# Eighty presorted chunks in place of sixty-three in a graph-convolution kernel on one core

## The chip, the core and the metric

The kernel runs on one core of one Trainium2 chip. The number that counts is the device time of one execution in microseconds (us). Three runs of the kernel before took 5122.73, 5125.78 and 5127.1 us; the median is 5125.78 us. One more execution, of 5141.47 us, was recorded by the hardware profiler; every row of a profile below is of that one.

A core has five engines, each with its own queue of instructions that it works off in order: TensorE (PE, matmuls; PEld is its loading of weights), VectorE (DVE), ScalarE (ACT), GpSimd (POOL) and SyncE (SP, which here issues DMAs only). They wait for each other through semaphores.

## The reference

412,500 edges, sorted by destination `dst`, carry 20 features and a weight; 12,500 nodes carry 128 features. Cut to what matters:

```python
h    = relu(layernorm(x)) @ W_in2f
Wij  = (ssp(f_ij @ W_f1 + b_f1) @ W_f2 + b_f2) * rcut_ij[:, None]
x_ij = h[dst] * Wij                        # the message of an edge
agg  = segment_sum(x_ij, src, 12500)       # messages added up by source node
out  = x + ssp(agg @ W_o1 + b_o1) @ W_o2 + b_o2
```

`ssp` is softplus minus log 2. The edges come in the order of `dst`, so that `h[dst]` is nearly local; `src` is random, so that adding up by `src` is the hard part. The nodes lie in 98 blocks of 128 (`NBLK`).

## The kernel before

**Chunks and steps.** The edges are cut into 806 chunks of 512 (`NCH`), and a chunk into four tiles of 128 edges (`QT`). A Python function `step(k)` writes the instructions of one step of the pipeline; what it writes is the order on every engine (the schedule is manual). The order inside a step is the string `"TMHPRXEBCKSAVUZWJL"`, a letter for each part: M is the product of value and picked node (line 1069, one DVE instruction for each chunk, the best clock of the steps), H the scaling of the picked rows on ACT (1056), P picks `h[dst]` with four matmuls (1040), R ranks the edges of a chunk (949, 921 on PE, 929 on DVE), X is one piece of the presort, C and S are the compares and the matmuls of the collection (1171, 1193), A and V make the value (1007, 1019), Z the hidden layer (878, or 874 for a sorted chunk), L its logarithm on ACT (884, 491, 492). Parts run ahead of their chunk: P of step k belongs to chunk k+2, Z to chunk k+4 at most, the loads of rows to chunk k+6 (`LW`).

**A chunk that is not sorted.** Its messages are scattered to a table in DRAM, so that the messages of one source block lie together: POOL issues four indirect DMAs for each chunk (1085), 128 rows of 129 floats each. The place of a row comes from the rank of its edge in its block, for which DVE marks the blocks (900), PE counts them (949, 921) and DVE takes the maximum (929). The first scatter of a chunk waits for a signal of PE in a later step (`PACED`).

**Segments and tiles.** The chunks form seven segments (`SEGS`; chunks 0 to 351, 352 to 527, 528 to 647, 648 to 703, 704 to 759, 760 to 791, 792 to 805). Each has a table with `T` tiles of 128 rows for each of the 98 blocks, and one more for the blocks whose own chunks lie in it. `T` is worked out from the mean number of messages of the chunks that are not sorted, with a margin of four standard deviations, and rounded up. When a segment is complete, its table is collected: SP loads a unit of up to six tiles (1151), DVE compares the stored place of each row with 0 to 127 (1171), and PE adds each tile into its block with one matmul (1193; it stands twice in a trace, since a 32-bit matmul is recorded as two). Segment 0 is collected from step 363 on. A small planner spreads all this work evenly over the steps that are left (`rate`, `jobs`): before, 9.12 tiles for each step in steps 371 to 658, 9.4 in 659 to 770, 10.9 in 771 to 804, and the rest behind the last chunk.

**A sorted chunk.** Some chunks (`SORT`, 63 of them: 57, 61, 65, ... 341, every fourth chunk, with a gap of eight after six or seven of them) are sorted by source block beforehand. The generator `sorting()` does it, piece by piece, four steps for each chunk, from step `PRE` = 18 on: PE ranks the 512 edges and permutes features, places and windows with matmuls against one-hot matrices (1372 to 1403), DVE makes these matrices (1396, 1399), ACT copies the result (1406), SP stores it (`s_rows` in 1407, `s_cols` in 1355, the latter one step later, when the next chunk's sort has begun). When the chunk's turn comes, SP loads the three pieces back (859, 860, 863), the features enter through three 16-bit matmuls (874), and the messages, which already lie in the order of blocks, go to `s_msgs` with one plain DMA of SP (1078). No rank, no marks, no scatters.

**Gathers.** Per block, one indirect DMA of POOL (1138) fetches the rows of that block from all sorted chunks: 128 places, each a run of `GR` = 6 consecutive messages. A chunk has one place by right (63), and where it has more than six edges of the block it takes further places (`EX` = 44 are kept for that). The indices of these runs are made by `indices()` after the last sort (44 DVE instructions in 1468, three in a step). A gather adds six tiles to the work of its block; the 98 gathers are dealt to the segments by their share of tiles (`extras`), and a gather is issued at the earliest four steps after the last sorted chunk and twelve steps before its compare (`EARLY`).

**What sets the order around the change.** The list `SORT` decides which chunks skip the scatter path; through `kept` in `Segment` it sets `T`, and through `T` the planner's `rate` and `jobs`. `PRE` says when the presort begins.

## Time and profile before

| | us |
|---|---|
| three runs | 5122.73, 5125.78 (median), 5127.1 |
| the profiled execution | 5141.47 |
| its span, first to last instruction | 5139.7 |
| PE busy | 3898.2 |
| DVE busy | 3190.8 |
| POOL busy | 3022.7 |
| ACT busy | 2716.1 |
| granted TensorE clock, mean | 0.868 of full speed |

The page gives busy times over the whole span. The span has stages with different work, so the stretches of time are what has to be read: there is one product (line 1069) for each chunk, and the number of these in a window divides its length into steps. The page's part on the chain that ended last is empty for this execution; what bounds a stretch has to be read from windows and waits. In a row of groups stand line, engine, operation, output and inputs, shapes and count; then busy time and the mean of one; then the idle time in front of it and what ended it.

### The profile page before, as it was taken

What the parts mean: (1) busy time and instruction counts of PE and PEld (TensorE: products, weight loads), DVE (VectorE), ACT (ScalarE), POOL (GpSimd) and SP (SyncE); (2) the same over time, 40 slices, a digit from 0 to 9 for tenths busy, and PEclk for the clock granted to TensorE, in tenths of its full rate; (3) what the DMA queues carried; (4) which work ended last, traced back from release to release, by engine and by line L of the source; (5) the groups of instructions that cost most, each with busy time, mean ns of one, the idle gap of its engine ahead of it and who ended that gap; (6) DMA issues with size and microseconds to landing.
All of it is one profiled execution on the core that took longest, in us unless ns stands there. A gap on an engine that the chain in (4) does not pass through costs nothing.

```text
span 5139.7 us, 78367 instructions
## 1 busy us (share of the span) xinstructions
PE 3898.2 (76%) x24234; PEld 2985.5 (58%) x24234; DVE 3190.8 (62%) x7496; ACT 2716.1 (53%) x6890; POOL 3022.7 (59%) x3168
## 2 busy tenths in 40 slices
PE   5677777777676566878888887888888778787879
PEld 3444544454444344666666666666666666666667
DVE  5666666666566444555655655665666666666757
ACT  6556666666666555445445444444444444444423
POOL 5665555555555556666666566666666665666643
PEclk8788888888887778988889898988999999999989
DMA  4556666666554454555565555566555655565647
GB/s 148 157 168 194 184 200 185 179 185 166 142 139 132 136 159 150 180 186 181 183 212 187 174 175 178 172 214 198 175 180 185 214 188 167 180 206 160 198 135 222
DMA packets 570652, 909.02 MB, mean 177 GB/s; under 512 B 160072, under 2 KB 349526, under 8 KB 570224
## 3 DMA queue, kind: packets, MB, share of 16 engines
q1 hardware_dynamic: 466050, 668.14, 43.8%
q0 software_dynamic: 102912, 235.26, 13.9%
q8 instruction: 193, 3.16, 0.3%
q14 instruction: 235, 1.93, 0.1%
q10 hardware_dynamic: 1262, 0.52, 0.0%
HBM read 499.23 MB, written 404.34 MB: 176 GB/s over the span
## 4 chain that ended last, share of the span: by engine, by line


## 5 line engine op out<-in xcount | busy, mean ns | idle before, releaser
L1085 POOL DMA_INDIRECT slots<-o,slot x2971 | 2871.8, 967 | 1885.6 <-issue 1345.1
L884 ACT ACTIVATE a<-z,bf 128x512 f32<-128x512 f32 x806 | 555.9, 690 | 1897.6 <-remote 738.3
L1069 DVE TENSOR_TENSOR o<-v,hg 128x512 f32<-128x512 f32 x806 | 555.2, 689 | 1189.0 <-issue 589.7
L1193 PE MATMUL sums<-to,m 128*128 128x128 f32 x8700 | 1222.8, 299 | 81.0 <-issue 73.2
L1193 PEld LDWEIGHTS sums<-to,m 128*128 128x128 f32 x8700 | 1191.3, 214 | 153.1 <-issue 122.0
L1019 PEld LDWEIGHTS v<-wf,r 128*128 128x128 f32 x6448 | 989.3, 219 | 495.7 <-issue 444.0
L1019 PE MATMUL v<-wf,r 128*128 128x128 f32 x6448 | 995.3, 303 | 36.8 <-issue 31.9
L1056 ACT ACTIVATE hg<-v,rcut 128x128 f32<-128x128 f32 x2972 | 837.6, 365 | 187.7 <-remote 94.2
L878 PE MATMUL z<-f,wf1z 128*128 128x512 f32 x1486 | 844.5, 649 | 61.1 <-issue 42.7
L1171 DVE TENSOR_TENSOR to<-counts,m 128x640 f32<-128x640 bf16 (+4 forms) x812 | 607.2, 782 | 358.8 <-remote 172.6
L1040 PEld LDWEIGHTS <-at 126*128 126x128 bf16 x2964 | 228.8, 104 | 808.2 <-issue 464.7
L1007 PE MATMUL v<-hb 128*128 128x512 bf16 x784 | 336.2, 429 | 352.2 <-DVE o L1069 274.9
L891 DVE SCALAR_TENSOR_TENSOR r<-z,nbf,a 128x512 f32<-128x512 f32 x806 | 598.1, 742 | 2.6 <-ACT a L492 2.1
L492 ACT ACTIVATE a<-a,half 128x512 f32<-128x512 f32 x806 | 581.9, 722 | 26.2
L929 DVE TENSOR_REDUCE top<-counts 128x4 f32<-128x392 f32 x743 | 414.4, 558 | 262.3 <-remote 197.3
L1040 PE MATMUL v<-near,at 126*128 126x128 bf16 x2964 | 321.9, 233 | 321.5 <-DVE at L999 149.5
L491 ACT ACTIVATE a<-a 128x512 f32<-128x512 f32 x806 | 508.0, 630 | 25.5
L949 PE MATMUL counts<-inb,rest_of 128*128 128x392 f16 x736 | 265.8, 361 | 317.5 <-issue 156.5
L878 PEld LDWEIGHTS z<-f,wf1z 128*128 128x128 f32 x1486 | 253.9, 211 | 68.5 <-issue 50.6
L921 PE MATMUL counts<-inb,after 128*128 128x392 f16 x743 | 271.9, 366 | 17.4 <-issue 16.5
L921 PEld LDWEIGHTS <-after 128*128 128x128 f16 x743 | 75.7, 102 | 358.5 <-issue 357.0
L999 DVE TENSOR_SCALAR at<-rel,prow 126x512 bf16<-126x512 bf16 x741 | 268.6, 362 | 0.0
(240 smaller groups left out, 2622.3 us busy)
## 6 DMA issues: line engine op xcount, KB each, us to landing
m<-slots SPq DMA_DIRECT2D x374, 322.5 KB
rel<-rel_d SPq DMA_DIRECT2D x201, 504.0 KB
m<-slots SPq DMA_DIRECT2D x238, 258.0 KB
m<-slots SPq DMA_DIRECT2D x147, 387.0 KB
f<-in_f_t SPq DMA_DIRECT2D x100, 512.0 KB
slots<-o,slot POOLq DMA_INDIRECT x2971
slots<-zero SPq DMA_DIRECT2D x100, 387.0 KB
slots<-zero SPq DMA_DIRECT2D x58, 516.0 KB
```

The lines of the kernel that those rows point to most:

```text
L491: nc.scalar.activation(a, a, AF.Exp, scale=-1.0)
L492: nc.scalar.activation(a, a, AF.Ln, bias=half, scale=0.5)
L878: kept["mm"] = nc.tensor.matmul(z_ps[k % 2], wf1z[:, k, :], self.f, start=True, stop=True)
L884: nc.scalar.activation(self.a[k], z_ps[k % 2], AF.Abs, bias=bf1)
L891: nc.vector.scalar_tensor_tensor(self.r[k], z_ps[k % 2], nbf1, self.a.pop(k), op0=ALU.max, op1=ALU.add)
L1019: mm = nc.tensor.matmul(v[:, i, :], r[:, i * P:(i + 1) * P], wf2, start=False, stop=True, skip_group_check=True)
L1040: mm = nc.tensor.matmul(ps[:, i, :], at[:, i * P:(i + 1) * P], near, start=i == 0, stop=i == QT - 1, skip_group_check=True)
L1056: act = nc.scalar.activation(hg[:, i, :], ps[:, i, :], AF.Copy, scale=cut[:, i:i + 1])
L1069: nc.vector.tensor_mul(self.o[c][:, :, :P], v, hg)
L1085: put = nc.gpsimd.indirect_dma_start(out=views[j % VIEWS], out_offset=bass.IndirectOffsetOnAxis(ap=self.slot[:, j:j + 1], axis=0), in_=o[: ...
L1171: nc.vector.tensor_tensor(to[:, :n, :], count_ps[:, None, :].to_broadcast([P, n, P]), m[:, :n, P:].to_broadcast([P, n, P]), op=ALU.is_equal)
L1193: kept["mm"] = nc.tensor.matmul(self.acc[b // QT][:, i, :], m[:, j, :P], to[:, j, :], start=t == 0, stop=t == self.tiles(b) - 1)
```

## The change

The list of sorted chunks becomes 33, 37, 41, ... 357 (72 chunks, with the same spacing as before) and 365, 373, ... 421 (eight more, every eighth chunk): 80 in all. With them 48 second runs fill the 128 places of a gather exactly. `PRE` goes from 18 to 14. In segment 0, 282 chunks are not sorted where 289 were, in segment 1, 166 where 176 were, and `T` comes out as 13 where it was 14, and as 8 where it was 9; the other segments keep theirs. `GJ`, the number of runs one chunk may have in a block, goes from 6 to 5. `both`, an intermediate, is held in 16 bits, and two small buffers move to another tile, since 80 chunks need more room. The new rule on `extras` gives segment 0 gathers only in even blocks from 62 on, 18 in place of 37; the segments behind it take the others.

```diff
-SORT = tuple(57 + i * 23 // 20 * 4 for i in range(63))
+SORT = tuple(33 + i * 23 // 20 * 4 for i in range(72)) + tuple(365 + 8 * i for i in range(8))
 NS = len(SORT)
 GR = 6
-GJ = 6
-EX = 44
+GJ = 5
+EX = 48
...
+LATE = 62
...
-PRE = 18
+PRE = 14
...
-            first_i = ra[:, 2 * cols:2 * cols + NS].bitcast(I32)
-            first_f = ra[:, 2 * cols + NS:2 * cols + 2 * NS]
...
-            both = rb[:, cols:3 * cols].rearrange("p (c k) -> p c k", k=2)
+            both = rb[:, cols:2 * cols].bitcast(BF16).rearrange("p (c k) -> p c k", k=2)
...
+            first_i = w3[:, 2 * RW:2 * RW + NS].bitcast(I32)
+            first_f = w3[:, 2 * RW + NS:2 * RW + 2 * NS]
...
-            total, start = bank[:nb, 200:201], bank[:nb, 256:256 + NS]
+            total, start = bank[:nb, 220:221], bank[:nb, 256:256 + NS]
...
-            i = max(range(len(share)),
+            i = max((i for i in range(len(share)) if i or b >= LATE and b % 2 == 0),
                     key=lambda i: share[i] * (b + 1) / sum(share) - len(extras[i]))
```

The lines of the changed kernel are one higher than those before, from the constants on.

What the table does to the order is seen in three places. The first is PE in step 31, which picks the rows of chunk 33. Before, behind the last of the four picks (`at` is the window of a chunk that is not sorted) come the two matmuls of the rank, then a piece of the presort (`nall`, `tri`), then bias, value and hidden layer of the next chunks:

```order
L1040 LDWEIGHTS at
L1040 MATMUL v_159<-near,at 128x128
L949 LDWEIGHTS rest_of
L949 MATMUL counts<-inb,rest_of 128x392
L921 LDWEIGHTS after
L921 MATMUL counts<-inb,after 128x392
L1388 LDWEIGHTS nall
L1388 MATMUL sums_158<-tri,nall 128x392
L1007 LDWEIGHTS hb_76
L1007 MATMUL v_160<-hb_76 128x512
L1019 MATMUL v_160<-wf_63,r 128x128 x4
```

In the changed kernel the same place reads (`sorted` is the tile with the presorted data):

```order
L1041 LDWEIGHTS sorted
L1041 MATMUL v_159<-near,sorted 128x128
L1389 LDWEIGHTS nall
L1389 MATMUL sums_158<-tri,nall 128x392
L1008 LDWEIGHTS hb_76
L1008 MATMUL v_160<-hb_76 128x512
L1020 MATMUL v_160<-wf_63,r 128x128 x4
```

The two matmuls of the rank are gone from this step; nothing else moved.

The second place is SP at the first load of sorted data. Before, chunk 57 is loaded (859, 860, 863) behind the store of the sixth sort's columns, so that its own five stores lie far back:

```order
L852 DMA near<-h_2_100 126x128
L1355 DMA s_cols<-pre_1313 128x8
L1921 DMA slots_129<-zero 96x1032
L859 DMA sorted<-s_rows 63x512
L860 DMA sorted<-s_rows 126x1x512
L863 DMA sorted<-s_cols 128x8
L241 DMA xb<-in_x 128x4x128
```

In the changed kernel chunk 33 is loaded directly behind the store of its own columns, the first that there is:

```order
L853 DMA near<-h_1_99 126x128
L1356 DMA s_cols<-pre_1136 128x8
L1922 DMA slots_129<-zero 96x1032
L860 DMA sorted<-s_rows 63x512
L861 DMA sorted<-s_rows 126x1x512
L864 DMA sorted<-s_cols 128x8
L1922 DMA slots_129<-zero 96x1032
L796 DMA f<-in_f_t 128x2x512
```

The load has moved from five sorts behind its own sort to right behind it, with the load of features (`f`) next in the queue.

The third place is PE in step 448, in the stretch in which segment 0 is collected. Before:

```order
L921 LDWEIGHTS after
L921 MATMUL counts<-inb,after 128x392
L1193 MATMUL sums_158<-to,m 128x128 x9
L1007 LDWEIGHTS hb_76
L1007 MATMUL v_160<-hb_76 128x512
L1019 MATMUL v_160<-wf_63,r 128x128 x4
L878 MATMUL z_155<-f,wf1z 128x512
```

And in the changed kernel:

```order
L922 LDWEIGHTS after
L922 MATMUL counts<-inb,after 128x392
L1194 MATMUL sums_157<-to,m 128x128 x8
L1008 LDWEIGHTS hb_76
L1008 MATMUL v_160<-hb_76 128x512
L1020 MATMUL v_160<-wf_63,r 128x128 x4
L879 MATMUL z_155<-f,wf1z 128x512
```

Eight tiles are added in this step in place of nine. Counted over the whole program, 4,468 tiles become 4,272: 297 fewer in steps 363 to 658, 53 more in 659 to 770, 24 more in 771 to 804 and 24 more behind the last chunk. Scatters go from 2,971 to 2,903, the stores and loads of sorted data from 63 to 80 sets.

## The prediction

> **What bounds the kernel now.** I read the page first: no engine is busy for more than 76% of the span, and the chain of waits is empty, so the bound has to be found stretch by stretch.
>
> ```profile
> PE 3898.2 (76%) x24234; PEld 2985.5 (58%) x24234; DVE 3190.8 (62%) x7496; ACT 2716.1 (53%) x6890; POOL 3022.7 (59%) x3168
> PEclk8788888888887778988889898988999999999989
> ```
>
> PE's granted clock steps up in the middle of the span, where segment 0 begins to be collected. So I cut the time at the steps where the work changes: chunks 33 to 56 (sorting has begun, no sorted chunk yet), 57 to 277 (sorted chunks and sorting), 278 to 340 (sorted chunks, no more sorting), 341 to 362 (neither), 371 to 658, 659 to 770 and 771 to 804 (collection at three rates). The windows view of line 1069, one instruction for each chunk, gives the length of a step in each:
>
> ```profile
> 222.30:370.80 148.50, 16.50 (x24) 0.78 0.56 162
> 370.80:1557.10 1186.30, 152.89 (x222) 0.82 0.62 175
> 1557.10:1895.90 338.80, 42.81 (x62) 0.78 0.48 140
> 1895.90:2028.00 132.10, 15.21 (x22) 0.77 0.41 128
> 2077.80:3989.30 1911.50, 198.48 (x288) 0.90 0.58 186
> 3989.30:4742.30 753.00, 77.09 (x112) 0.92 0.60 188
> 4742.30:4981.80 239.50, 23.39 (x34) 0.91 0.52 159
> ```
>
> Columns: window, its length, busy DVE with the count, granted PE clock, DMA share, GB/s. Dividing: 6.19, 5.34, 5.46, 6.00, 6.64, 6.72 and 7.04 us for a step. Two things stand in these rows. Without collection a step costs 6.0 to 6.2 us when no chunk is sorted, and 5.3 to 5.5 when 22% are; whether the presort itself runs (the second row) or not (the third) makes no difference. And with collection a step grows with its tiles, which the same view of line 1193 counts (two records a tile):
>
> ```profile
> 2077.80:3989.30 1911.50, 752.62 (x5272) 734.41 (x5272) 0.90 0.58 186
> 3989.30:4742.30 753.00, 287.64 (x2097) 283.60 (x2096) 0.92 0.60 188
> 4742.30:4981.80 239.50, 104.83 (x746) 101.06 (x747) 0.91 0.52 159
> ```
>
> That is 9.15, 9.36 and 10.97 tiles a step. The windows of all engines and the waits say who sets the pace there:
>
> ```profile
> 1895.90:2028.00 132.10, 81.01 (x373) 53.47 (x373) 58.93 (x138) 70.04 (x176) 83.43 (x86) 0.77 0.41 128
> 2077.80:3989.30 1911.50, 1549.75 (x10182) 1260.66 (x10181) 1153.66 (x2391) 928.53 (x2332) 1170.85 (x1215) 0.90 0.58 186
> ACT a L884 <- remote: 262.4, 61, 7.7
> ACT a L884 <- PE counts L921: 206.5, 68, 6.7
> ACT a L884 <- PE z L878: 202.0, 58, 8.2
> ```
>
> The first two rows give PE, PEld, DVE, ACT and POOL; the other three are waits in the window 2077.8 to 3989.3. In the collection PE is busy 81% (1549.75 of 1911.5), POOL and DVE 61 and 60%; ACT stands for results of PE, and PE is last. Before the collection (first row) nobody is above 63%; a step is a round of waits between PE, DVE, ACT and POOL there.
>
> **The change part by part.** The sum is made against the profiled execution (span 5139.7, whole 5141.5 us); the median of the runs is 0.997 of it, which changes a sum of some 80 us by 0.3, so I subtract from the median directly.
>
> *Sorted chunks before the collection.* Chunks 33 to 56 get six and chunks 341 to 362 four; between 57 and 340 there are 62 where there were 63. I take the step of the mixed stretch, (1186.3 + 338.8) / 284 = 5.37 us: 24 x (6.19 - 5.37) = 19.7, 22 x (6.00 - 5.37) = 13.9, together 33.6. The one chunk lost costs a sorted chunk's worth: 0.63 to 0.82 us a step at 22% sorted is 2.8 to 3.7 us a chunk, say 3.3. Term: **-30 us**. Bounds: 9 chunks net x 2.8 = -25, x 3.7 = -33. The mechanism is not PE's work alone: what a sorted chunk drops is four scatters, the rank and two DVE instructions, against a hidden layer of three 16-bit matmuls:
>
> ```profile
> L1085 POOL DMA_INDIRECT slots<-o,slot x2971 | 2871.8, 967 | 1885.6 <-issue 1345.1 <-PE v L1019 126.1 <-ACT a L884 83.4
> L878 PE MATMUL z<-f,wf1z 128*128 128x512 f32 x1486 | 844.5, 649 | 61.1 <-issue 42.7 <-DVE r L891 14.5 <-DVE inb L900 1.6
> L929 DVE TENSOR_REDUCE top<-counts 128x4 f32<-128x392 f32 x743 | 414.4, 558 | 262.3 <-remote 197.3 <-PE v L1040 18.0 <-issue 17.7
> L921 PE MATMUL counts<-inb,after 128*128 128x392 f16 x743 | 271.9, 366 | 17.4 <-issue 16.5 <-DVE top L929 0.5 <-DVE used L955 0.4
> L949 PE MATMUL counts<-inb,rest_of 128*128 128x392 f16 x736 | 265.8, 361 | 317.5 <-issue 156.5 <-DVE top L929 145.3 <-remote 2.1
> L874 PE MATMUL z<-sorted,wst 63*128 63x512 bf16 x189 | 75.1, 522 | 0.0
> ```
>
> On PE that is 0.37 + 0.36 (rank) and 844.5 / 743 = 1.14 against 75.1 / 63 = 1.19 us: 0.68 us less. The rest of the 3.3 us is the round through DVE (929, for which the next 949 waits 145.3 us in all) and POOL's 3.9 us of scatters.
>
> *Seventeen more sorts.* I cost them at nothing. They fall into steps 278 to 342, and there PE has over a third of its time free (211.27 of 338.8 us busy, first row below); the second and third rows of the first windows show that such free time takes a sort (5.34 with, 5.46 without). If that cover were gone, PE's larger part of a sort,
>
> ```profile
> 1557.10:1895.90 338.80, 211.27 (x1061) 139.32 (x1060) 180.06 (x488) 196.35 (x500) 191.90 (x196) 0.78 0.48 140
> L1403 PE MATMUL sums<-pre,pre_d 128*107 128x512 bf16 x252 | 83.8, 465 | 0.0
> L1377 PE MATMUL sums<-pre,ones 128*128 128x294 f16 x189 | 33.4, 295 | 0.7 <-issue 0.7
> L1468 DVE SCALAR_TENSOR_TENSOR early_room<-early_room 98x378 f32<-98x378 f32 x44 | 24.3, 552 | 1.0
> ```
>
> (83.8 + 33.4) / 63 = 1.9 us, would cost 17 x 1.9 = 32 us. The indices (last row; four more, 48 x 0.55 = 27 us of DVE) move to steps 343 to 364, still ahead of the first sums; DVE is busy 45% there (58.93 of 132.1). Seventeen more stores and three times seventeen loads on SP, and 68 fewer indirect DMAs and 30 fewer clears, go with it. Starting four steps earlier costs nothing that I can find a row for.
>
> *Fewer tiles.* 297 fewer in steps 363 to 658, 101 more behind. The price of a tile has four readings. PE's own busy time, 752.62 / 2636 = 0.286 us. The third rate against the first, (7.04 - 6.64) / (10.97 - 9.15) = 0.22. The second against the first, 0.08 / 0.21 = 0.4, too short a lever. And the chord down to the stretch without any tiles, (6.64 - 6.00) / 9.15 = 0.07. The change goes from 9.12 tiles to 8.12 and up to 10 and 11.6, near the rows with 9 to 11, so I take 0.22, the one reading between two stretches of the same clock (0.90 and 0.91) with a lever of almost two tiles: -297 x 0.22 = -65, +101 x 0.22 = +22. Term: **-43 us**. Bounds: 0.35 throughout, towards the second reading, -69; the chord going down (-21) and 0.286 going up (+29), +8.
>
> The low price has a reason in the rows: PE's granted clock is 0.77 where PE is busy 61% and 0.90 where it is busy 81%, so taking work from PE also takes some of its clock. [...]
>
> *Sorted chunks in the collection.* Eight, from 365 to 421. PE sets the pace there, so each is worth at least its 0.68 us, and at most the 3.3 of the early stretch. Nearer to the first, since POOL and DVE are not last: 1.2 each. Term: **-10 us**, bounds -5 and -26.
>
> *Gathers dealt differently.* 98 as before; in segment 0 they start later, and 54 lie behind step 658 where 37 did. Their tiles are in the count above; DVE's compare of one,
>
> ```profile
> L1165 DVE SCALAR_TENSOR_TENSOR to<-m,counts 128x768 f32<-128x768 f32 x98 | 92.7, 946 | 39.5 <-remote 19.8 <-PE z L878 11.2 <-PE v L1019 5.7
> ```
>
> is 0.95 us on an engine that is idle 40% there. Nothing.
>
> **Sum**: -30 - 43 - 10 = -83 us: 5125.8 - 83 = **5043 us**, 1.6% faster.
>
> **The rivals.** *The clock takes the tiles back.* In the collection, fewer tiles make PE idle oftener, its clock falls towards 0.77, and a step stays near 6.6; only the chord's 0.07 us a tile is won, while the later, fuller steps pay 0.286. For it: the no-tile stretch takes 6.00 us a step with half the matmuls (373 / 22 = 17 records a step against 10182 / 288 = 35). Against it: the third rate shows 0.22 a tile at the same clock (0.91). Time: -25 + 8 - 5 = -22, **5104 us**.
>
> *More than the sum.* The early mechanism, less of POOL and DVE in the round, holds in the collection too, and a tile is worth 0.35, between the first and the second reading: -33 - 69 - 26 = -128, **4998 us**.
>
> *Slower: the sorted data come too late.* Before, the first sorted tile is loaded five sorts after its own sort:
>
> ```profile
> L859 SPq DMA_DIRECT2D sorted<-s_rows x63: 286/403/1511, 336.2 to 1852.4; - x63
> L874 PE MATMUL z<-sorted,wst x189: 376/603/631, 350.4 to 1878.2; 63*128 63x512 bf16 x189
> SPq L1407 <- ACT pre L1406: 223.0, 25, 17.8
> ```
>
> The load is issued at 336.2 us and PE uses it at 350.4, 14.2 us later. In the changed kernel the load of chunks 33 to 57 (seven of them, spaced like the sorts) stands right behind the store of its own columns, SP is held by the sort (the last row is a wait of SP between 180 and 1600 us: up to 17.8 us for ACT's copy), and behind the load in SP's queue stand features and windows of later chunks. The store has to land, then the load, within some 14 us. If PE has to stand for it, it decides once seven stalls outweigh the gain, at 83 / 7 = 12 us each; at 15 us each it is +105 - 83, **5148 us**. Against it: the issue of these DMAs takes 0.4 to 0.9 us each, and the store's wait is for a copy that PE's order puts two steps ahead of the use.
>
> **How the numbers follow.** The forecast 0.58, the clock rival 0.20, more than the sum 0.12, late data 0.10. The likeliest one's own range is 5015 to 5075. The range for eight in ten reaches to both neighbours, 4998 to 5106, and leaves out late data, half of what the clock rival has above its number and a little below the other. A measurement of this kernel can tell 0.2%, 10 us, from no change: faster 0.58 + 0.12 + most of the clock rival 0.16 = 0.86, within 0.05, slower 0.09.
>
> **What would show it.** Steps of 5.4 us in chunks 33 to 56 and 341 to 362; 8.1 tiles and 6.4 us a step in 371 to 658 with PE's clock at 0.88 to 0.90, 6.85 us in 659 to 770 and 7.2 in 771 to 804; the clock rival would show 6.55 or more in the first of these and a clock of 0.85. Late data would show as steps over 7 us between chunks 33 and 57, with PE waiting for a DMA of `sorted`. The forecast is wrong if the first collection stretch stays above 6.5 us, or if the stretch after step 278, now with sorting, is slower than 5.5.

## The result, and the profile after

In twelve runs of each the changed kernel took 5097.14 us (5080.24 to 5110.1), the kernel before 5114.74 us (5101.87 to 5134.72). The ratio is 0.9961 [0.9945, 0.9978]: 0.4% faster, some 20 us, where 83 were forecast. The profiled execution of the changed kernel is the fastest of its twelve (5080.24 us) and that of the kernel before the slowest of all (5141.47 us). Their 61 us of difference are therefore mostly chance; single stretches vary too (steps 278 to 340 took 325 to 344 us in seven kernels that are the same there), and where it matters I use several kernels.

The page of the changed kernel: its engines, the granted clock of PE in 40 slices, and POOL's scatters.

```profile
PE 3908.5 (77%) x24114; PEld 2965.9 (58%) x24114; DVE 3200.6 (63%) x7639; ACT 2722.9 (54%) x6941; POOL 2957.1 (58%) x3100
PEclk8887878888777878999988988898999999898889
L1086 POOL DMA_INDIRECT slots<-o,slot x2903 | 2806.1, 967 | 1819.1 <-issue 1287.3
```

There are 68 scatters fewer (2971 to 2903), and each occupies POOL for 967 ns as before. The clock is as it was. The windows of all engines follow, cut at the same steps as in the prediction: 33, 57, 278, 341, 363, then 515, 659 and 771 to 805. The columns are the window, its length, busy PE, PEld, DVE, ACT and POOL with counts, granted clock, DMA share and GB/s. First the changed kernel, then three rows of the kernel before for the same steps as the last three.

```profile
220.70:347.20 126.50, 87.86 (x530) 59.15 (x530) 92.82 (x287) 84.65 (x224) 70.07 (x72) 0.88 0.67 196
347.20:1526.30 1179.10, 863.28 (x4855) 583.90 (x4855) 781.68 (x2158) 766.09 (x2023) 669.22 (x691) 0.80 0.60 171
1526.30:1859.10 332.80, 240.36 (x1345) 159.43 (x1344) 200.42 (x516) 209.36 (x557) 194.72 (x200) 0.80 0.56 157
1859.10:1972.80 113.70, 73.75 (x372) 48.66 (x372) 81.99 (x250) 69.93 (x178) 67.47 (x68) 0.81 0.42 125
1972.80:2336.10 363.30, 306.61 (x2038) 244.79 (x2037) 226.99 (x485) 198.80 (x501) 207.89 (x216) 0.93 0.63 199
2915.90:3871.50 955.60, 752.59 (x4788) 603.72 (x4787) 565.09 (x1208) 460.00 (x1158) 586.90 (x609) 0.90 0.55 176
3871.50:4643.40 771.90, 622.41 (x4126) 501.17 (x4126) 488.49 (x1003) 354.98 (x898) 465.68 (x483) 0.92 0.59 186
4643.40:4913.00 269.60, 211.65 (x1350) 172.92 (x1349) 161.59 (x327) 103.09 (x262) 145.88 (x152) 0.86 0.49 150
```

```profile
3036.70:3989.30 952.60, 772.49 (x5090) 627.62 (x5091) 584.43 (x1214) 459.55 (x1157) 583.78 (x606) 0.90 0.58 185
3989.30:4742.30 753.00, 594.57 (x3993) 485.00 (x3991) 478.06 (x987) 353.56 (x892) 453.62 (x470) 0.92 0.60 188
4742.30:4981.80 239.50, 193.58 (x1305) 159.69 (x1304) 156.62 (x319) 103.25 (x266) 139.96 (x145) 0.91 0.52 159
```

In steps: 5.27 us in chunks 33 to 56 (6.19 before), 5.17 in 341 to 362 (6.01), 5.28 in 278 to 340, where the presort now runs (5.45 without it). So far it went as forecast. From step 515 to 658 PE's records fall from 5090 to 4788, which is one tile a step, and its busy time by 20 us, but the window is not shorter: 6.62 us a step before, 6.64 after. Behind step 658 the steps are longer: 6.72 to 6.89 and 7.04 to 7.93 us.

### The profile page after: what moved, and what is told of

Same layout as the page of the kernel before. It is cut to its first block, busy times and chain, and to the rows that moved or that the text cites. A ratio compares the mean times of both kernels' runs of the same rounds, so it can differ in the third digit from the quotient of the medians.

```text
span 5078.5 us, 78295 instructions
## 1 busy us (share of the span) xinstructions
PE 3908.5 (77%) x24114; PEld 2965.9 (58%) x24114; DVE 3200.6 (63%) x7639; ACT 2722.9 (54%) x6941; POOL 2957.1 (58%) x3100
## 4 chain that ended last, share of the span: by engine, by line
## 5 line engine op out<-in xcount | busy, mean ns | idle before, releaser
L1086 POOL DMA_INDIRECT slots<-o,slot x2903 | 2806.1, 967 | 1819.1 <-issue 1287.3
L1194 PE MATMUL sums<-to,m 128*128 128x128 f32 x8296 | 1200.0, 299 | 181.1 <-issue 168.9
L1194 PEld LDWEIGHTS sums<-to,m 128*128 128x128 f32 x8296 | 1142.9, 213 | 267.5 <-issue 229.6
L1020 PEld LDWEIGHTS v<-wf,r 128*128 128x128 f32 x6448 | 1002.7, 221 | 440.9 <-issue 383.1
L1020 PE MATMUL v<-wf,r 128*128 128x128 f32 x6448 | 1005.8, 305 | 49.4 <-issue 41.4
L1057 ACT ACTIVATE hg<-v,rcut 128x128 f32<-128x128 f32 x2904 | 818.9, 366 | 152.1 <-remote 83.5
L879 PE MATMUL z<-f,wf1z 128*128 128x512 f32 x1452 | 812.1, 641 | 40.2 <-DVE r L892 19.8
L1172 DVE TENSOR_TENSOR to<-counts,m 128x512 f32<-128x512 bf16 (+3 forms) x824 | 582.7, 740 | 347.9 <-remote 129.5
L930 DVE TENSOR_REDUCE top<-counts 128x4 f32<-128x392 f32 x726 | 403.9, 556 | 213.6 <-remote 148.9
L1041 PE MATMUL v<-near,at 126*128 126x128 bf16 x2896 | 308.8, 232 | 257.4 <-DVE at L1000 133.3
```

The lines of the kernel that those rows point to most:

```text
L879: kept["mm"] = nc.tensor.matmul(z_ps[k % 2], wf1z[:, k, :], self.f, start=True, stop=True)
L1020: mm = nc.tensor.matmul(v[:, i, :], r[:, i * P:(i + 1) * P], wf2, start=False, stop=True, skip_group_check=True)
L1041: mm = nc.tensor.matmul(ps[:, i, :], at[:, i * P:(i + 1) * P], near, start=i == 0, stop=i == QT - 1, skip_group_check=True)
L1057: act = nc.scalar.activation(hg[:, i, :], ps[:, i, :], AF.Copy, scale=cut[:, i:i + 1])
L1086: put = nc.gpsimd.indirect_dma_start(out=views[j % VIEWS], out_offset=bass.IndirectOffsetOnAxis(ap=self.slot[:, j:j + 1], axis=0), in_=o[: ...
L1172: nc.vector.tensor_tensor(to[:, :n, :], count_ps[:, None, :].to_broadcast([P, n, P]), m[:, :n, P:].to_broadcast([P, n, P]), op=ALU.is_equal)
```

## The experiments

**The change taken apart.** Four kernels tell the three parts of the change from each other. `late_gathers` is the kernel before with the new dealing of the gathers only; `late_tiles` has in addition the changed kernel's fewer tiles (with 63 sorted chunks, so its tables have less margin); `sorted_only` is the changed kernel with the tiles of the kernel before; `level` is the changed kernel with all gathers in segments 0 to 2.

```diff
+LATE = 62                                                     # late_gathers
-            i = max(range(len(share)),
+            i = max((i for i in range(len(share)) if i or b >= LATE and b % 2 == 0),
+            if k < 2:                                         # late_tiles: late_gathers, and
+                self.T = (13, 8)[k]
+            if k < 2:                                         # sorted_only: the changed kernel, and
+                self.T = (14, 9)[k]
-LATE = 62                                                     # level: the changed kernel, and
+LATE = 48
-        share = [sum(seg.tiles(b) for b in range(NBLK)) for seg in segs[:-1]]
+        share = [sum(seg.tiles(b) for b in range(NBLK)) for seg in segs[:3]]
-            i = max((i for i in range(len(share)) if i or b >= LATE and b % 2 == 0),
+            i = max((i for i in range(len(share)) if i or b >= LATE),
```

> The kernel before with the changed rule for the gathers alone (18 in segment 0, in even blocks from 62 on), so that 91 tiles move from steps 363-658 to later ones: 8.8, 9.9 and 11.6 tiles a step in 371-658, 659-770 and 771-804 where it was 9.1, 9.4 and 10.9. Theory K (knee): below some 9 tiles a step is held at 6.6 us by the round of a chunk that is not sorted, so tiles taken away there win nothing, while above it a tile costs 0.4 us and more: steps of 6.6, 6.9 and 7.8 us, 40 to 50 us slower than before. Theory L (a tile is worth 0.22 us everywhere, as the prediction had it; the profile of the changed kernel is off by chance): within 10 us of before.

> The same, and with 13 and 8 tiles a block in segments 0 and 1 in place of 14 and 9, with the 63 sorted chunks of before (their messages fit): the tiles of the changed kernel (8.1, 9.9, 11.6 a step) without its sorted chunks. Theory K: steps of 6.6, 6.9 and 7.8 us as in the kernel with the gathers moved alone, 40 to 50 us slower than before. Theory L: 196 tiles at 0.22 us, 43 us faster than before.

> The changed kernel with 14 and 9 tiles a block as before: its 80 sorted chunks and its gathers, without the 196 tiles less. Theory K: the time of the changed kernel within 10 us (17 to 20 us faster than before), since the tiles were worth nothing. Theory L: 43 us slower than the changed kernel, 25 us slower than before.

> The changed kernel with its gathers dealt to segments 0 to 2 only, and in segment 0 from block 48 on, so that the tiles are level: 8.8, 9.4 and 9.5 a step in 371-658, 659-770 and 771-804. Theory K: the later stretches fall to 6.7 us a step, the first stays at 6.6: 40 to 50 us faster than the changed kernel, 60 faster than before. Theory L: the same number of tiles, so the time of the changed kernel within 10 us.

Measured against the kernel before on the same chip (5126.89 us): `late_gathers` 1.0096 [1.0078, 1.0115], 49 us slower; `late_tiles` 1.0056 [1.0040, 1.0073], 29 slower; `sorted_only` 0.9983 [0.9970, 0.9997], 9 faster; `level` 0.9906 [0.9885, 0.9926], 48 faster, 28 more than the change itself. The differences give the other two parts twice (the ratio of the changed kernel is that of the first runs): the dealing of the gathers costs 49 us; 196 tiles fewer win 20 (`late_tiles` against `late_gathers`) or 11 (the changed kernel against `sorted_only`), 0.06 to 0.10 us a tile; the 17 sorted chunks win 58 or 49. By the intervals of the ratios each difference is good to some 12 us, so that the tiles are clear of 0.22 us each, which would be 43 us, but hardly of nothing. The sum 49 - 15 - 54 = -20 comes to the result by construction, since the changed kernel is one of its ends. Theory K came nearest, though it had the tiles at nothing and `level` at 60 us. So a part that I had priced at nothing took most of the gain, and moving gathers once more gave it back.

**Does a gather cost by the buffer that it holds?** In the trace a gather is issued 82 us ahead of its compare and keeps one of the 11 buffers of the ring `m` for that time. Three kernels shorten that lead from 12 steps to 5, one lengthens it to 22.

```diff
-EARLY = BACK + 2
+EARLY = 5                 # late_short, after_short, level_short
+EARLY = 2 * BACK + 2      # before_long
```

> The kernel before with the changed dealing of the 98 gathers (which by itself cost 49 us), and each gather issued 5 steps ahead of its compare in place of 12. Theory H (hold): a gather takes one of the 11 buffers of the ring m when it is issued and keeps it until its tiles are summed, 82 us in the traces; moved behind step 658 they are 4.2 at a time there where they were 2.8, and the plain loads have fewer buffers. With 5 steps it is 1.8 at most: 5116 to 5136 us, within 10 of the kernel before. Theory P (the gather itself: its time on POOL, its DMA) and theory U (a gather breaks the grouping of small blocks into one load and one compare, 80 units a segment where 72 were) leave the hold out: 5165 to 5180, still 40 to 50 slower.

> The changed kernel with each gather issued 5 steps ahead in place of 12. Theory H: the 49 us that the moved gathers cost come back: 60 to 75 us faster than the kernel before. Theories P and U: as the changed kernel, 10 to 30 faster than before.

> The variant with all gathers in segments 0 to 2, 48 us faster than the kernel before, with each gather issued 5 steps ahead. Its gathers held 5.3 buffers between steps 425 and 545. Theory H: that cost goes too, 60 to 90 us faster than before, and within 15 us of the changed kernel with the short hold. Theory U: 40 to 55 faster, as with the long hold, and 20 to 35 faster than the changed kernel with the short hold. Theory P: as U.

> The kernel before with each gather issued 22 steps ahead in place of 12, so that it holds a buffer almost twice as long (4.7 at a time in place of 2.6); nothing else moves. Theory H: 30 to 60 us slower than before. Theories P and U: within 10.

These ran on another chip, and there the kernel before took 4056.93 us, not 5126.89. Its granted clock was 0.96 where the chips so far gave 0.87. Against the kernel before on that chip: `late_short` 1.0054 [1.0041, 1.0067], `after_short` 0.9865 [0.985, 0.9879], `level_short` 0.9783 [0.9771, 0.9796], `before_long` 0.9973 [0.9963, 0.9983]. Holding a buffer longer costs nothing there: theory H fell on that chip (0.3% the other way is more than chance, and I have no cause for it). On chips with 0.87 the lead was not changed, but `level` speaks against H there too: its gathers hold 5.0 buffers at a time in steps 425 to 514 and none in 771 to 804, those of the kernel before 2.6 and 2.9, and yet what a step has beyond POOL's own time (worked out below) is 1.26 and 1.57 us in `level`, 1.31 and 1.62 before. A shorter lead does harm, for a row among the waits for the tile `m` in `late_short`:

```profile
  DMA m<-s_msgs,idx: 172.4, 43
```

DVE stands 172 us for gathers that land late; POOL had issued them about one step ahead of their compare, where the program says five. POOL was behind by some four steps, and that led to the next reading.

**POOL sets the pace on the chips with 0.96.** The groups of POOL in steps 515 to 658, first of the kernel before in the profile of the prediction, then of a kernel on the chip with 0.96 (`half_sums`, below; the same on POOL):

```profile
L1085 POOL DMA_INDIRECT slots<-o,slot x576 | 554.0, 962 | 341.2 <-issue 280.6 <-ACT a L884 37.1 <-DVE inb L900 11.6
L1138 POOL DMA_INDIRECT m<-s_msgs,idx x30 | 29.8, 994 | 28.5 <-remote 10.4 <-PE counts L921 8.4 <-issue 5.5
```

```profile
L1085 POOL DMA_INDIRECT slots<-o,slot x579 | 559.2, 966 | 176.5 <-issue 122.5 <-DMA slots<-o,slot 11.9 <-ACT a L491 4.0
L1138 POOL DMA_INDIRECT m<-s_msgs,idx x30 | 29.6, 985 | 9.1 <-issue 5.2 <-PE counts L921 1.5 <-PE v L1019 0.6
```

The columns are count, busy time, mean ns of one, and the idle time before them with what ended it. In the second fence busy and idle, 588.8 + 185.6 us, fill the window of 773.6 us, and the idle time is the same small gap 609 times: 185.6 / 609 = 0.305 us. POOL takes 0.967 us for an indirect DMA, and the next begins 0.305 us later: 1.27 us each. In the profiles of the kernel before and of the changed kernel no indirect DMA begins less than 0.299 us behind another. No gap of POOL is over 0.35 us from step 363 to 804 there. At its 76% of busy time POOL is full.

On the chips with 0.87 the median gap is the same 0.305 us, but the idle time is twice as long: 369.7 - 606 x 0.305 = 185 us are left, 1.28 us a step, in pauses. From the records of the kernel before in this window: 91 pauses of POOL over 1 us, 2.3 us in the mean, one every 10.5 us, and in them the others work less too (PE busy 65% in place of 86%, DVE 47 for 65, ACT 27 for 54). The pauses stand in front of the first scatter of a chunk (79) or of a gather (12), never in front of the three scatters that follow. The first scatter starts 7.5 us behind the start of its chunk's product there (median, 1.1 steps; the program has it one step later), in `before_long` on the chip with 0.96 43.5 us, 8.1 steps. So on 0.87 POOL has no work in store: it waits for its chunk again and again and is not full, whereas on 0.96 it always has a queue. I write every step as its indirect DMAs times 1.27 us, and a remainder (3.96; 1.15 is 3.96 x 1.27 + 1.15 = 6.19 us):

| steps | before | changed | late_again | before_split | before_plain | late_plain | level |
|---|---|---|---|---|---|---|---|
| 33-56 | 3.96; 1.15 | 3.00; 1.45 | 4.12; 1.08 | 4.04; 1.07 | 4.04; 1.12 | 4.12; 1.05 | 3.04; 1.84 |
| 363-424 | 4.21; 1.25 | 3.47; 1.45 | 3.97; 1.08 | 4.23; 1.08 | 3.98; 1.11 | 4.00; 1.07 | 3.48; 1.59 |
| 515-658 | 4.21; 1.26 | 4.23; 1.26 | 4.24; 1.14 | 4.20; 1.15 | 4.01; 1.13 | 4.00; 1.13 | 4.29; 1.33 |
| 659-770 | 4.20; 1.38 | 4.31; 1.41 | 4.31; 1.56 | 4.21; 1.27 | 3.98; 1.24 | 4.00; 1.55 | 4.12; 1.45 |
| 771-804 | 4.26; 1.62 | 4.44; 2.28 | 4.35; 2.19 | 4.21; 1.41 | 4.06; 1.78 | 4.06; 1.89 | 4.06; 1.57 |

The kernels of the four middle columns come next. On the chips with 0.96 the remainder is within 0.04 us of nothing from step 363 to 804 in all ten kernels that ran there. POOL's share of busy time does not show that: in steps 515 to 658 of `half_sums` 76% was the limit, since the gap of 0.305 us behind an indirect DMA is not in it.

**The gather taken from POOL.** Four kernels on a chip with 0.87 (before: 5046.42 us). Two replace a gather's indirect DMA by a plain one of SP; one only splits the small blocks of the late segments.

```diff
-                load = nc.gpsimd.indirect_dma_start(      # before_plain; and in late_gathers: late_plain
-                    out=m.rearrange("p t f -> p (t f)")[:, :GR * RW], out_offset=None,
-                    in_=s_msgs[:, :],
-                    in_offset=bass.IndirectOffsetOnAxis(ap=idx[:, b:b + 1], axis=0))
+                load = nc.sync.dma_start(
+                    m.rearrange("p t f -> p (t f)")[:, :GR * RW],
+                    s_msgs[b * P:b * P + P * GR, :].rearrange("(p t) f -> p (t f)", t=GR))
-                             and not any(i in extra for i in range(b, b + n)))     # before_split
+                             and not any(i in extra or i in apart for i in range(b, b + n)))
...                           (`apart`: the blocks that the new dealing would take alone)
```

> The kernel before with the changed dealing of the 98 gathers alone, once more, as the mark for the next three. On a chip that grants a clock of 0.87, 40 to 55 us slower than the kernel before, as in the first run; on one that grants 0.95, where POOL sets the pace, 10 to 30 slower, from the variant with the short hold.

> The same, but each gather's load is one plain DMA on SP of as many bytes from the stored messages of the sorted chunks, at the same step into the same buffer, in place of an indirect DMA on POOL; its compare and its six sums stay. (The rows that it loads are others, so the second runs' messages are missing from the sums.) Theory P (the gather on POOL holds up the scatters): the cost of dealing them late is gone, within 10 us of the same plain loads dealt as before. Theory U (more tiles and units in the late segments): 40 to 50 slower than those.

> The kernel before, with its gathers replaced by plain loads on SP in the same way. Theory P: 15 to 60 us faster than the kernel before, 98 times 0.15 to 0.6. Theory U: within 10.

> The kernel before, in which small blocks of the late segments are loaded and compared one by one wherever the changed dealing would do so (227 units in the last three segments in place of 203), with every gather where it was. Theory U: 24 more units at 0.9 us (the regression over the stages of six kernels), 15 to 30 us slower. Theory P: within 6.

`late_again` 1.0118 [1.0097, 1.014], 60 us slower; `late_plain` 0.986 [0.9838, 0.9882], 71 faster; `before_plain` 0.9789 [0.9766, 0.9812], 106 faster; `before_split` 1.0021 [1.0005, 1.0038], 11 slower. Without POOL a gather is 106 / 98 = 1.1 us cheaper, dealt late 131 / 98 = 1.3, which is the size of POOL's 1.27; `before_plain` won almost twice the most that theory P allowed. One stretch shows it alone, steps 515 to 658 with the same 9.12 tiles; first `before_split`, then `before_plain`:

```profile
2976.10:3910.60 934.50, 772.98 (x5081) 626.67 (x5082) 585.62 (x1214) 459.82 (x1157) 583.01 (x605) 0.91 0.60 188
```

```profile
2933.50:3831.20 897.70, 745.28 (x5071) 604.25 (x5072) 583.96 (x1218) 457.52 (x1159) 555.21 (x578) 0.94 0.62 197
```

The window is 36.8 us shorter for 27 indirect DMAs fewer, 1.36 us each, with the matmuls as they were. So an indirect DMA taken from POOL counts in full at the lower clock too, although POOL is not full there. How it holds up the step is not shown, nor is it told apart from the other queue that the load then takes.

Neither theory had the cost of dealing late whole: U had 15 to 30 us for `before_split`, P none for `late_plain`. With plain loads it is still 38 us (4973.49 against 4935.27), with indirect ones 60. The rows of steps 659 to 770, `before_plain` and then `late_plain`:

```profile
3831.20:4537.90 706.70, 587.26 (x4018) 472.71 (x4017) 478.06 (x987) 353.51 (x892) 428.58 (x447) 0.94 0.64 201
```

```profile
3823.60:4566.80 743.20, 605.73 (x4112) 494.22 (x4110) 487.35 (x1002) 356.29 (x896) 431.46 (x449) 0.93 0.63 196
```

POOL does the same (447 and 449), there are 47 tiles more (94 records), and the step goes from 6.31 to 6.64 us. Splitting the units does not do it: `before_split` has a remainder of 1.27 there. So behind step 658 the remainder grows where gathers, with their tiles, are added. With the old dealing (9.4 tiles) it is 1.24 to 1.38 in 659 to 770, with the new one (9.9) 1.41 to 1.65 in six kernels, the profile of the changed kernel being the lowest; in 771 to 804 it is 1.4 to 1.8 at 10.9 tiles and 1.9 to 2.3 at 11.6. In steps 515 to 658, from 9.1 to 8.1, it does not move (1.26 and 1.26). Whether it is the number of tiles, with a knee somewhere above 9.4, or the gathers themselves (each also brings a compare and a load; 659 to 770 have 32 or 33 in place of 24, 771 to 804 12 in place of 8) no run tells apart, since none changes the tiles alone there. `level` fits neither quite: 1.45 at 9.3 tiles and 22 gathers, 1.57 at 9.5 tiles and none. What is shown is that gathers moved behind step 658 take POOL's time and more with them, and that their tiles won nothing where they were taken away. Moving the gathers out of 771 to 804 altogether shows the other side; `late_again`, then `level` (with 80 sorted chunks, and on another chip; the changed kernel took 269.6 us, as shown above):

```profile
4691.20:4953.90 262.70, 204.35 (x1336) 167.05 (x1334) 160.42 (x324) 103.48 (x261) 143.47 (x149) 0.87 0.51 152
```

```profile
4713.90:4942.70 228.80, 182.38 (x1203) 148.22 (x1201) 148.44 (x303) 103.85 (x266) 132.55 (x138) 0.90 0.50 155
```

These 34 steps are 34 us shorter, and the stretch from the last message to the end is 141.6 us in `level` against 156.8 before and 164.5 in the changed kernel, where nine gathers lie in place of five.

**Do the sums set the pace anywhere, and what is a sorted chunk worth?** `half_sums` leaves out every second sums matmul of the kernel before. In `sorted_scatter` the 18 sorted chunks that the change adds at the two ends of the sorted stretch and in the collection, and chunk 341, which was sorted before, scatter their messages as well, into tables that nothing reads. `even` deals the gathers to the first three segments as 36, 35 and 27.

```diff
+                    if self.seg is not segs[-1] and t % 2 and t < self.tiles(b) - 1:   # half_sums
+                        continue
+                    if k in PLUS:                                                      # sorted_scatter
+                        more = [nc.gpsimd.indirect_dma_start(
+                            out=scrap[PLUS.index(k)][i][:, :],
+                            out_offset=bass.IndirectOffsetOnAxis(ap=pidx_i, axis=0),
+                            in_=o[:, i, :], in_offset=None) for i in range(QT)]
...                                              (paced as the other scatters are)
-LATE = 48                                                                  # even: level, and
+LATE = 44
-            i = max((i for i in range(len(share)) if i or b >= LATE),
+            i = max((i for i in range(len(share)) if i or b >= LATE and b % 3),
```

> The kernel before without every second sums matmul of a block in the collection of segments 0 to 5 (loads, compares and gathers stay; the sums are wrong by what is left out): some 4 of 9 matmuls a step fewer. Theory K (floor and knee: below some 9 tiles a step is held by the chunk's own round through POOL, above them PE sets it): steps 515 to 658 stay within 0.3 of 6.5 to 6.6 us, steps 659 to 770 fall by 0.3 to 0.6, 771 to 804 by 0.7 to 1.2; in all 80 to 180 us faster than before. Theory L (a tile costs 0.22 to 0.29 us of PE everywhere): 0.9 to 1.2 us a step throughout, 400 to 530 us faster.

> The changed kernel, where the 19 sorted chunks at 33 to 53, 341 to 357 and 365 to 421 also scatter their messages with four indirect DMAs each into tables that nothing reads, paced as the other scatters are; rank and search stay out. Theory S (what a sorted chunk saves is its four scatters on POOL): the whole gain of these chunks goes, 45 to 60 us slower than the changed kernel, with steps of 6.2 in 33 to 56 and 6.3 in 363 to 424. Theory R (it saves the rank on PE and the round through DVE): within 12 of the changed kernel.

> The changed kernel once more, as the mark for the others on the same chip: 10 to 30 us faster than the kernel before where the granted clock is 0.87.

> The changed kernel with the 98 gathers dealt to segments 0 to 2 as 36, 35 and 27, where the variant that was 48 us faster than before had 47, 29 and 22. If a gather costs the same wherever POOL sets the step (1.2 to 1.9 us, from the plain loads), the same 48 within 10. If crowding costs (0.44 a step in steps 425 to 514 there, 0.34 here), 55 to 70 faster than before.

They ran on a chip with 0.96 (before: 4060.17 us): `half_sums` 0.9991 [0.9982, 1.0], `sorted_scatter` 1.0021 [1.0012, 1.003], `after_again` 0.9819 [0.9804, 0.9835], `even` 0.9762 [0.9749, 0.9776]. The forecasts had the figures of chips with 0.87 in mind: `half_sums` was to win 80 us at the least, `even` 48 to 70 where it won 97, and that of `after_again` did not apply. Steps 515 to 658 of `before_long` (which is the kernel before but for the gathers' lead), then of `half_sums`:

```profile
2346.00:3115.20 769.20, 690.89 (x5075) 567.52 (x5074) 586.49 (x1216) 455.60 (x1157) 584.71 (x606) 0.98 0.74 229
```

```profile
2337.80:3111.40 773.60, 612.99 (x3915) 463.43 (x3915) 588.47 (x1219) 457.00 (x1162) 588.30 (x609) 0.94 0.73 228
```

Four matmuls a step fewer, 1160 records, are worth nothing, although PE was busy 90% of the time with them; POOL's 1.27 x 606 = 770 and 1.27 x 609 = 773 us are the windows. PE's granted clock is 0.98 in the first row and 0.94 in the second, where PE has less work; it changes no time here. For a sorted chunk, steps 363 to 424 of `after_again`, then of `sorted_scatter`:

```profile
1502.50:1777.10 274.60, 268.23 (x2034) 222.27 (x2034) 230.03 (x488) 199.99 (x502) 208.77 (x217) 1.00 0.86 262
```

```profile
1526.00:1844.10 318.10, 282.22 (x2040) 229.53 (x2039) 230.57 (x484) 198.53 (x504) 241.57 (x252) 0.97 0.79 234
```

With the scatters put back, and rank and search still left out, the eight chunks cost 43.5 us, 5.4 each; four scatters are 5.1 (POOL does 35 more indirect DMAs in the window, three more than the eight chunks have). In all `sorted_scatter` is 81 us slower than the changed kernel on that chip: the whole gain, theory S, and more than the 45 to 60 that S had said; 76 scatters x 1.27 us are 97. And on that chip the change wins 73 us [67, 80]. That follows from POOL alone: 68 scatters x 1.27 = 86 us less, and the end behind the last message is 14 us longer (165.1 us against 151.1 in `before_long`).

The last two were meant for a chip with 0.87 and met one with 0.96 again (before: 4070.93 us).

> The kernel before without every second sums matmul in the collection, for a chip that grants 0.87. If PE's sums set the step at that clock (theory L, 0.22 to 0.29 us a tile): 0.9 to 1.2 us a step, 400 to 530 us faster than before, down to POOL's 5.35 us a step at the most (that is 570). If a step below nine tiles is held by the chunk's own round (theory K): 0 to 0.3 us a step in 515 to 658, 80 to 180 us faster in all. On a chip that grants 0.96: no difference, as in the first run.

> The changed kernel, where the 19 added sorted chunks also scatter. On a chip that grants 0.87: with theory S (a sorted chunk saves its scatters) 45 to 60 us slower than the changed kernel, so 25 to 40 slower than before; with theory R (it saves the rank and the round through DVE) within 12 of the changed kernel, so 8 to 32 faster than before. On a chip that grants 0.96: 8 slower than before, as in the first run.

`half_again` 1.0 [0.9991, 1.0009], as in the first run, on a second chip of that clock. `scatter_again` 1.005 [1.0036, 1.0064] is 20 us slower than before, where the first run was 8 slower; the changed kernel itself did not run on this chip. Whether half of the sums would be free at 0.87 too, and whether a sorted chunk saves its scatters alone there, was not measured.

## Why the prediction was wrong

The forecast was -30 - 43 - 10 = -83; the parts measured some -31, -15, -22 and +49. These parts are shown; why a tile is cheap and a late gather dear at 0.87 is shown in part only.

- *Sorted chunks before the collection*, -30: right. Over the kernels with 63 and with 80 sorted chunks on chips with 0.87 the means are 150.0 against 132.6 us in steps 33 to 56 and 126.6 against 113.5 in 341 to 362, together -30.5, where 33.6 was forecast, and steps 57 to 277 do not change (1168.8 to 1181.5 against 1174.9 to 1183.6), so the lost chunk's 3.3 cannot be seen. (Chunk 341 was sorted before, so the counts are 61 against 62 chunks between 57 and 340, and one in the stretch 341 to 362; the term stays.) The reason given, the round through DVE with POOL's scatters as a part of it, was too wide where the clock is 0.96: it is the scatters, 4 x 1.27 = 5.1 us each. At 0.87 the gain is that less what the remainder grows by, and the two reasons were not told apart.
- *Seventeen more sorts*, 0: right. Steps 278 to 340 took 334 us with them and 332 without (means of three and seven).
- *Fewer tiles*, -43: the step that failed first, with its price of 0.22 us. Measured were 0.06 to 0.10. I took the lever between 9.15 and 10.97 tiles for the price of going from 9.1 to 8.1. It lies in another stretch; in steps 515 to 658 a tile is free (6.62 and 6.64 us). The chord, 0.07, was the better reading. What misled was reading the bound from busy shares: "PE is last" with 81% against POOL's 61%. The row of line 1085 that stands in the prediction had the missing part: 1345.1 of 1885.6 us of idle time before the scatters with nothing to wait for, of which 2971 x 0.305 = 906 us are the gap behind each. With it POOL sets the step alone where the clock is 0.96, and half of the sums are free; at 0.87 its time counts too, but what else holds the step stays open.
- *Gathers dealt differently*, "Nothing": the step that failed most. 49 us on one chip, 60 on another. Seventeen gathers moved behind step 658 carry 17 x 1.27 us of POOL, 102 tiles, and their compares and loads to stretches that pay for more than POOL's time; what they leave behind wins the POOL time only. I had counted their tiles in the term above, at +22, and set only DVE's compare against the rest.
- *Sorted chunks in the collection*, -10: right in sign, too small. 20 to 24 us for eight (`sorted_only` against `late_gathers`, the changed kernel against `late_tiles`), 2.5 to 3.0 each in place of 1.2; "POOL is not last" was the error again. On the chips with 0.96 it is 5.4.

Steps 371 to 658 took 6.43 us in the mean, as forecast (6.4), but not for the reason: 5.86 up to 424, for sorted chunks and missing gathers, and 6.64 from 515 on, with the fewer tiles. Steps 771 to 804 took 7.93 where 7.2 was forecast. So the sign that was to show the forecast wrong, a first collection stretch above 6.5 us, did not come: it was too coarse, since it mixes stretches that went both ways.

Of the rivals, *the clock takes the tiles back* named a step that stays near 6.6 and 5104 us, and both came: 6.64, and 0.9961 x 5126 = 5106. Its mechanism was not the one. The clock in that stretch is 0.90 with 9.1 tiles and with 8.1, not 0.85, and where the clock is 0.96 the tiles are free as well. Its time was met by luck: sorted chunks and tiles won some 46 us more than it had (68 in place of 22), and the dealing of the gathers, which it did not have, cost 49. *Slower: the sorted data come too late* is refuted: no step of 33 to 56 is held (5.27 us), and among the waits for the tile `sorted` in the changed kernel stands

```profile
  DMA sorted<-s_rows: 0.7, 1
```

one wait of 0.7 us for its rows in the whole run.

What stays open: what a chunk waits for in the pauses that make up the remainder of 1.1 to 1.4 us on the chips with 0.87, why POOL's time counts there although POOL is not full, and what makes the remainder grow behind step 658. With them goes why 86 us of POOL's time turned into 20 there: by the table and the row of steps 341 to 362 the remainder takes back 7 (33 to 56), 4 (341 to 362), 12 (363 to 424), 3 and 22 us (behind 658), and the end 8, together 56 of 86, which leaves 30 against the 20 of the medians. The two profiled executions lie 61 us apart; most of the other 31 us fell in steps 278 to 340 (11) and 425 to 514 (19), and is at least in part chance. That the remainder grows where POOL has less to do fits pauses in which POOL would catch up if it had a store of work, as it has on the chips with 0.96; this was not tried.

Two versions beat both kernels: `level` on a chip with 0.87 (48 us faster than before, the change 20), `even` on one with 0.96 (97, the change 73). Neither was run at the other clock (`level_short`, which is `level` with the short lead, was 88 faster than before at 0.96), and `even` beats `level` by nothing that was measured side by side.

## What to carry to other kernels

Before an engine is called free by its busy share, divide a stretch of the trace by the count of its instructions, and count a gap that stands behind each of them as a part of it: here 0.305 us behind each indirect DMA, with which POOL, busy 76% of the time, set the pace in `half_sums`. Whether it did showed in how far it ran behind the work that it was given: 8.1 steps in `before_long`, where it set the pace alone, 1.1 in the kernel before, where it did not. A price for work taken away is to be read in the stretch that it is meant for: 0.22 us a tile from other stretches became 0.06 to 0.10. And work that is "only dealt differently" has the same total but not the same place: count what the places that receive it are already short of.

## What the chips showed that I had not expected

- The same kernel took 5046 to 5127 us on chips where PE's records show a granted clock of 0.87 and 4057 to 4071 us where they show 0.96, a quarter more. Steps without any collection differ as much (5.35 and 4.08 us in 57 to 277). The page of `before_long` on the faster one:

```profile
PEclk9989998999998989999999999999999999999999
```

- So one change had two results: 0.9961 [0.9945, 0.9978] where pauses are added to POOL's time, 0.9819 [0.9804, 0.9835] where, in the collection, POOL's time is all there is.
- A scatter of 128 rows of 516 bytes took POOL 0.966 to 0.967 us in the mean on chips of both clocks, with a gap of 0.305 us behind it; a gather of 3096 bytes a row took nearly the same, 0.98 to 0.99 us.
